# Scores of four key tiles by 512 queries as 26 products instead of two times 14, in 7 of 12 groups

## The chip, the cores and the metric

The kernel runs on one core of one Trainium2 chip, as one program. The metric is the device time of one execution in microseconds (us). A core has a matrix engine (PE) with its weight load (PEld), a vector engine (DVE), a scalar engine (ACT), a general engine (POOL), and SP, which here only issues DMAs. Each engine works through its own queue in the order in which the program wrote it; an instruction that waits holds up everything behind it on that engine. DMAs are issued from the queues of SP and POOL.

## The reference

There are 3327 nodes with 512 features (26 tiles of 128 rows, the last one with 127), and one adjacency matrix. First two rounds of attention over all nodes, then a layer norm, then a binarised layer, then another layer norm:

```python
for l in range(2):
    Wh, Ws = jnp.split(x @ W_stack[l], 2, axis=-1)      # W_stack[l] is 512 by 1024
    a = jax.nn.softmax(Wh @ Ws.T, axis=-1) * adj
    x = leaky_relu(a @ Wh + x, 0.01)
x = layernorm(x0 + x)
x = layernorm(x + relu(adj @ (max(sign(x), 0) @ sign(weight).T)))
```


W_stack is 2 by 512 by 1024. Everything up to the first layer norm is float32. The change concerns the scores `Wh @ Ws.T` of both rounds.

## The kernel before

**The scores as a product of 512 by 512.** With M, the product of the two halves of the weights, a score is a bilinear form of the key's and the query's x. In the stage `project(l)` the kernel makes the query side M x once, in 7 chunks `c` of 512 queries (the last has 256), and in the stage `attention(l)` it multiplies it by the key tiles. For one pair of key tiles `q` (256 keys, 13 pairs) and one chunk, the product is taken as a 2 by 2 block scheme of Strassen's kind: seven block products instead of eight. The left factors ("forms" of the keys) are four raw blocks and four sums (`A11 A12 A21 A22 S1..S4`, of which seven are used), the right ones are `B11 B21 B22 T1..T4`. Each block product has depth 256, that is, two calls of `nc.tensor.matmul` of 128 by 128 by 256. So a pair costs 14 matmul calls, and two pairs (four key tiles) cost 28. Each float32 matmul call stands in the profile as two MATMUL instructions.

**Stage one, `project(l)`.** A chunk `c` is a `weave` of lists: the query side (`queries`, two chains `seven(...)`), the values of two pairs (`project_values`, two chains of `seven`), and `turns`, which are DVE transposes of the next chunk's x (`turn_x`), key sums of the next chunk (`key_sums`), and `prepare` (sums of the next chunk's right factors). `weave` spreads every list evenly over the chunk. Key forms, query forms and value forms are stored to DRAM (`xs_d`, `gs_d`, `ws_d`) by DMAs from the POOL queue: six per pair of key tiles in `keys`, seven per chunk in `queries`.

**Stage two, `attention(l)`.** Two orders run side by side. `steps` is the list of (g, q), 13 groups g of 256 queries by 13 key pairs; step v takes the values: `shift` (subtract the column maximum, DVE), `exponential` (ACT), `running` (sum, DVE), `masked` (times adjacency, DVE), `sums` (four POOL operations of 128x128), then `values`, seven matmul calls into PSUM accumulators. `ahead` is the list of (c, q, s), two half-steps per chunk and key pair; it makes the scores `LOOK` = 30 steps earlier. The loop runs over v, with u = v + LOOK; from v = 0 on, one pass holds seven value matmul calls and eight or six score matmul calls. Within a pass, each operation has a fraction, and `sorted(work, ...)` sets the order in which it is written into every queue: for example `shift` at 0.0, `running` at 0.01, `exponential` at 0.12, `masked` at 0.4, `narrow` (ACT), `degrees` (POOL) and `exact` (DVE) at 0.6 to 0.62 in every second pass, and the scores at

```python
return [(0.06, z1), (0.31, x2), (0.45, add11), (0.56, z6), (0.81, y5)]          # s == 0
return [(0.02, z7), (0.2, add22), (0.35, y3), (0.5, add12), (0.68, z4), ...]    # s == 1
```

The passes with u from 0 to 29 come before v = 0, so they hold scores but no values; they are the scores of chunk 0 and the beginning of chunk 1, in each of the two rounds. The chunk c = 6 has only 256 queries, so its score matmuls are 128 wide.

**How a score leaves PSUM.** The seven products of a pair use three PSUM banks, Z, X and Y (pool `ps_ch`, three buffers). The bank Z is added to by four products in turn; after each, `copied` takes its state out by an ACT copy, and the next product into Z waits for that copy. Per pair there are five ACT copies (three out of Z on the way, one of Y, one as c21) and three DVE adds (`add11`, `add22`, `add12`). Then `maximum` (DVE, 128x512) takes the finished score tile into the column maximum, twice per pair. Score tiles are slots of the ring `s` (`SBUFS` = LOOK + 3).

**Loads.** `load_xs` fetches a pair's key forms two passes ahead (two DMAs, 512 and 384 KB), `load_gs` the next chunk's query forms one by one (double-buffered tile `gs`, 14 KB per partition each), `load_ws` the value forms, `load_adj` the adjacency; all from SP.

## Time and profile before

| | before |
|---|---|
| median of 3 runs | 2530.15 us (2528.65 to 2535.02) |
| the profiled execution | 2530.58 us |
| its span in the profile | 2528.8 us |
| MATMUL instructions | 12237 |

The span is the time from the first to the last instruction on the core; the difference to the execution's time, 1.8 us, lies around it. By position in the span: the first projection ends at 185 us (first score product at 185.1), passes without values run to 277.7, the first round's value steps to about 1228; the second round's first score product is at 1387.5, its first value step at 1480.2, its last near 2423; then comes the binarised layer. In the attention rounds, four passes (two key pairs) take 24.1 to 24.4 us in a chunk of 512 queries, 18.3 to 18.7 us in the chunk of 256, and 12.1 us where there are no values.

A row of the profile's groups reads: line, engine, operation, output <- input, shape, count, busy time in all, mean ns of one, and the idle time of that engine just before it with what ended it. A windows answer gives for each stretch its length, then the busy time of each engine with the number of its instructions in brackets, the granted clock, the share of the DMA engines and GB/s.

### The profile page before, as it was taken

How to read it: one execution, taken by the hardware profiler on the slowest of the kernel's cores; microseconds unless marked ns; L12 is line 12 of the kernel's file. 1: busy time of each engine (PE TensorE's matmuls, PEld its weight loads, DVE VectorE, ACT ScalarE, POOL GpSimd, SP SyncE). 2: the span in 40 equal slices, each digit the busy share in tenths (PEclk: the TensorE clock that was granted, in tenths of full speed). 3: DMA queues.
4: the chain of work that ended last, by engine and by line, in shares of the span. 5: the costliest groups of instructions: out<-in, count | busy, mean ns of one | idle time of the engine just before them, and what ended most of it. 6: DMA issues, size and time to landing. Idle time of an engine off the chain costs nothing.

```text
span 2528.8 us, 39245 instructions
## 1 busy us (share of the span) xinstructions
PE 2505.6 (99%) x12237; PEld 2182.1 (86%) x12237; DVE 2024.0 (80%) x3749; ACT 784.2 (31%) x1822; POOL 1467.6 (58%) x2303
## 2 busy tenths in 40 slices
PE   9999999999999999999999999999999999999998
PEld 7888888888888888998888888888888888899875
DVE  5765778789787897869876587888888888898976
ACT  3323333333333233222232333332323323322234
POOL 3652566766666666556665256666666666655631
PEclk9999999999999999999999999999999999999999
DMA  6857777777767767798885877777777777778984
GB/s 206 298 199 236 229 248 232 247 250 238 248 231 250 246 231 246 249 315 267 256 295 204 254 232 249 244 251 254 239 260 238 255 248 242 248 261 301 316 283 151
DMA packets 311394, 628.83 MB, mean 249 GB/s; under 512 B 35819, under 2 KB 166755, under 8 KB 310924
## 3 DMA queue, kind: packets, MB, share of 16 engines
q1 hardware_dynamic: 278254, 529.13, 64.4%
q0 software_dynamic: 32896, 97.09, 10.4%
q8 instruction: 100, 1.64, 0.3%
q14 instruction: 114, 0.93, 0.1%
q10 hardware_dynamic: 30, 0.03, 0.0%
HBM read 528.54 MB, written 97.58 MB: 248 GB/s over the span
## 4 chain that ended last, share of the span: by engine, by line
PE 93%; DVE 4%; issue 1%; DMA 1%; POOL 1%; ACT 0%; SPq 0%; ACTq 0%; DVEq 0%; POOLq 0%
PE acc L830 37%; PE pZ L596 22%; PE pY L596 11%; PE pX L596 6%; PE pZ_wh L412 4%; PE pZ_g L474 3%; PE agg L1120 3%; PE pY_wh L412 2%; PE pY_g L474 2%; PE pm L316 1%; PE pxw L1212 1%; PE pX_wh L412 1%; PE pX_g L474 1%; DVE s L754 1%; PE pg L449 1%
## 5 line engine op out<-in xcount | busy, mean ns | idle before, releaser
L596 PE MATMUL pZ<-gs,xs 128*128 128x256 f32 (+1 forms) x2912 | 699.4, 364 | 0.6 <-ACT u L614 0.4
L596 PEld LDWEIGHTS pZ<-gs,xs 128*128 128x128 f32 x2912 | 536.2, 190 | 72.6 <-ACT p L614 1.3
L803 POOL TENSOR_TENSOR as<-s 128x128 f32<-128x128 f32 x338 | 169.1, 500 | 592.6 <-DVE s L770 411.5
L830 PE MATMUL acc<-ws,s 128*128 128x256 f32 x1352 | 402.2, 379 | 0.0
L596 PE MATMUL pY<-gs,xs 128*128 128x256 f32 (+1 forms) x1456 | 352.1, 364 | 1.8 <-ACT p L614 1.8
L830 PE MATMUL acc<-ws,as 128*128 128x256 f32 x1352 | 349.5, 380 | 2.0 <-POOL as L805 2.0
L830 PE MATMUL acc<-wh,s 128*128 128x256 f32 x1352 | 349.0, 379 | 0.0
L783 POOL TENSOR_TENSOR deg<-deg,adj 128x256 fp8e4<-128x256 fp8e4 x338 | 280.1, 829 | 52.0 <-DMA adj<-in_adjT_dram 37.6
L662 DVE TENSOR_TENSOR top<-top,s 128x512 f32<-128x512 f32 x286 | 248.1, 873 | 73.1 <-ACT s L649 70.5
L596 PEld LDWEIGHTS pY<-gs,xs 128*128 128x128 f32 x1456 | 268.3, 190 | 37.5 <-ACT p L614 2.6
L754 DVE TENSOR_TENSOR s<-s,off 128x512 f32<-128x512 f32 x338 | 296.0, 876 | 0.6
L830 PEld LDWEIGHTS acc<-ws,as 128*128 128x128 f32 x1352 | 251.2, 190 | 40.4 <-POOL as L805 4.7
L830 PEld LDWEIGHTS acc<-ws,s 128*128 128x128 f32 x1352 | 252.9, 190 | 32.2
L830 PEld LDWEIGHTS acc<-wh,s 128*128 128x128 f32 x1352 | 251.6, 190 | 33.5 <-DVE s L770 0.3
L760 ACT ACTIVATE s<-s 128x512 f32<-128x512 f32 x338 | 213.4, 631 | 194.9 <-DVE s L754 192.5
L765 DVE TENSOR_TENSOR total<-total,s 128x512 f32<-128x512 f32 x312 | 270.0, 865 | 0.0
L614 ACT COPY u<-pZ 128x256 f32<-128x256 f32 (+1 forms) x364 | 129.9, 357 | 422.8 <-PE pZ L596 417.5
L639 DVE TENSOR_TENSOR s<-p,u 128x256 f32<-128x256 f32 (+1 forms) x182 | 86.8, 477 | 215.4 <-ACT u L614 210.2
L770 DVE TENSOR_TENSOR s<-s,adj 128x512 f32<-128x512 f32 x338 | 246.4, 729 | 5.0
L804 POOL TENSOR_TENSOR s<-s 128x128 f32<-128x128 f32 x338 | 233.0, 689 | 26.9
L805 POOL TENSOR_TENSOR as<-s 128x128 f32<-128x128 f32 x338 | 225.4, 667 | 26.5
L806 POOL TENSOR_TENSOR as<-s,as 128x128 f32<-128x128 f32 x338 | 205.6, 608 | 26.5
(195 smaller groups left out, 3454.7 us busy)
## 6 DMA issues: line engine op xcount, KB each, us to landing
ws<-ws_d SPq DMA_DIRECT2D x338, 512.0 KB
xs<-xs_d SPq DMA_DIRECT2D x182, 512.0 KB
adj<-in_adjT_dram SPq DMA_DIRECT2D x351, 256.0 KB
xs<-xs_d SPq DMA_DIRECT2D x182, 384.0 KB
gs_d<-gsp POOLq DMA_DIRECT2D x84, 256.0 KB, 2.9
gs<-gs_d SPq DMA_DIRECT2D x70, 256.0 KB
xs_d<-xT POOLq DMA_DIRECT2D x104, 128.0 KB, 3.3
xs_d<-s POOLq DMA_DIRECT2D x52, 256.0 KB, 3.2
```

The lines of the kernel that those rows point to most:

```text
L412: nc.tensor.matmul(bank, of[LEFT[i]][:, k], wr[RIGHT[i]][:, k], start=(start and k == 0), stop=(k == 1), skip_group_check=True,)
L596: nc.tensor.matmul(ch[bank], xs[c, q, a][:, k], gs[c][:, b, k], start=(start and k == 0), stop=(k == 1), skip_group_check=True,)
L662: nc.vector.tensor_tensor(top[i], top[i], t, ALU.max)
L754: nc.vector.tensor_tensor(s, s, off[g].to_broadcast([P, 2, HW]), ALU.subtract)
L760: nc.scalar.activation(sc[g, q], sc[g, q], AF.Exp)
L765: nc.vector.tensor_tensor(total[g], total[g], sc[g, q], ALU.add)
L770: nc.vector.tensor_tensor(s, s, adj[g, q], ALU.mult)
L783: nc.gpsimd.tensor_tensor(deg[:, g], deg[:, g], adj[g, q][:, a], ALU.add, saturate=False)
L804: nc.gpsimd.tensor_tensor(a21, a21, a22, ALU.add)
L805: nc.gpsimd.tensor_tensor(s2, a21, a11, ALU.subtract)
L806: nc.gpsimd.tensor_tensor(s4, a12, s2, ALU.subtract)
L830: nc.tensor.matmul(acc[g][i // 2][:, i % 2], a[i], b[i], start=(q == 0 and i % 2 == 0), stop=(q == NQ - 1), skip_group_check=True,)
```

## The change

Seven of the 12 groups of four key tiles (`QUADS`: groups 1 to 4 in the first round, 1 to 3 in the second; a group is key pairs 2i and 2i+1) are computed for all seven chunks by another scheme. It has 26 products of depth 128, with left forms `x0` to `x25` and 26 right forms. 16 of the right forms are halves of the seven that exist (`QUERY`), and ten are new (`EXTRA`).

In `project`: the key pairs of such a group no longer store their eight blocks; `quad_sums` makes their forms with 24 POOL operations of 128x128 (`add`, `sub`) and six ACT copies (`one`, `whole`) per group, in the projection's chunk `c` whose key pairs are that group's (c = i), and stores them with two DMAs of 13 forms. `query_sums` makes the ten new right forms with ten DVE operations of 128x256 per chunk (128x128 in the last one) and stores them with five POOL DMAs. The last chunk's store and sums (`done`) and these sums go as `rest` into the next chunk's `turns`. Other pairs store three raw blocks rather than four.

In `attention`: `quad_scores` writes 26 matmul calls at 6.5 per pass over four passes, in the order `ORDER`, into five PSUM tiles P, Q, R, S, T of the same three buffers. Per group there are 17 ACT copies out of PSUM, two ACT copies back into PSUM (`seed`, into Q and P), seven DVE adds with an operand in PSUM (`out`), four DVE adds in SBUF, and four POOL adds of 128x256; the four maxima come at 4.75 to 6.35 passes after the group's start, which is during the next group. Forms are loaded 13 at a time in one DMA (852 KB), from a tile of 14 forms with two buffers. The query forms are in two single tiles `ga` (7) and `gb` (5), which change roles with each chunk: one holds the seven, the other the extras, `load_gs` runs in passes 20 to 24 of the chunk before and in pass 0, `load_ge` in passes 1 to 5. The ring gets two slots more, and the packed bits of the last stage move from a `gs` tile to ring slots.

```diff
+QUADS = ((1, 2, 3, 4), (1, 2, 3))
+ORDER = (11, 8, 3, 23, 14, 16, 12, 22, 9, 1, 25, 20, 4,
+         21, 13, 7, 19, 24, 6, 5, 15, 18, 2, 10, 17, 0)
...
-    SBUFS = LOOK + 3
+    SBUFS = LOOK + 5
...
+    def quad_sums(l, i, pair0, pair1):
...
+        def first():
+            sub(at["x3"], x_(A22, 1, 0), x_(A22, 0, 0))
+            sub(at["x22"], x_(S1, 0, 1), at["x3"])
...
+        def sixth():
+            add(at["x16"], x_(S1, 0, 0), at[4])
+            one(0, 10, x_(S2, 1, 0))
+            whole(0, 11, of[1][S3])
+            nc.gpsimd.dma_start(out=xq_d[l][i, 0], in_=staged[0][:, :13])
...
+    def query_sums(l, c, gs, b12):
...
+        def first():
+            sub(23, gs[B11][:, 0], gs[T3][:, 1])
...
+            store(0, 4)
...
+            if q // 2 in QUADS[l]:
+                return of
             to = xs_d[l][q]
-            for raw in (A11, A12, A21, A22):
+            for raw in (A11, A12, A22):
...
-                weave(one + two, pairs, turns)
+                quad = []
+                if c in QUADS[l]:
+                    quad = quad_sums(l, c, of_pair[2 * c], of_pair[2 * c + 1])
+                weave(one + two, pairs, turns, quad)
...
+        def quad_scores(c, i):
...
+            begins = {11: "P", 8: "Q", 3: "R", 24: "S", 10: "T"}
+            joins = dict(zip(
+                (23, 12, 1, 4, 7, 6, 18, 17, 14, 22, 25, 21, 19, 5, 2, 16, 9, 20, 13, 15, 0),
+                "PPPPPPPPQQQQQQQRRRRST",
+            ))
...
+            place = {r: (n + 0.5) / 6.5 for n, r in enumerate(ORDER)}
+            got = [(at_, lambda r=r: one(r)) for r, at_ in place.items()]
+            for r, b, name in (
+                (11, "P", "c10"), (8, "Q", "c21"), (23, "P", "c11"), (14, "Q", "c01"),
+                (16, "R", 1), (12, "P", "c31"), (22, "Q", 3), (9, "R", 2), (1, "P", "c30"),
+                (25, "Q", 0), (20, "R", 1), (4, "P", "c20"), (7, "P", "c00"), (24, "S", 2),
+                (6, "P", 3), (5, "Q", "c01"), (10, "T", 2),
+            ):
+                got.append((place[r] + 0.03, lambda b=b, name=name: keep_as(b, name)))
+            pool = nc.gpsimd
+            got += [
+                (1.0, lambda: add("c10", "c10", 1, pool)),
+                (1.15, lambda: add("c31", "c31", "c01", pool)),
+                (1.45, lambda: add("c11", "c11", 2, pool)),
+                (2.2, lambda: out("c10", "Q")),
+                (2.4, lambda: seed("Q", 3)),
+                (2.5, lambda: out("c00", "R")),
+                (2.82, lambda: add(0, 0, 2)),
+                (3.05, lambda: add("c00", "c00", 0, pool)),
+                (3.22, lambda: out("c20", "S")),
+                (3.38, lambda: out("c21", "P")),
+                (3.54, lambda: out("c11", "Q")),
+                (3.6, lambda: seed("P", "c30")),
+                (3.85, lambda: out("c30", "P", 0)),
+                (4.005, lambda: out("c31", "T")),
+                (4.1, lambda: add(1, 1, 3)),
+                (4.2, lambda: add("c21", "c21", 2)),
+                (4.3, lambda: add("c01", "c01", 1)),
+            ]
...
-            c, i = divmod(u - 7, 2 * NQ)
-            if 0 <= c < NC - 1 and i % 2 == 0 and i // 2 < 7:
-                load_gs(c + 1, i // 2)
+            c, i = divmod(u, 2 * NQ)
+            if 0 <= c < NC - 1 and 20 <= i < 25:
+                load_gs(c + 1, i - 20)
+            if 0 < c < NC and i == 0:
+                load_gs(c, 5, 2)
+            if 0 <= c < NC and 1 <= i < 6:
+                load_ge(c, i - 1)
```

## The prediction

> **What bounds the kernel now.** I read the engines' busy times and the chain first, then groups by shape, then stretches of the length of four passes, since the change acts on groups of four passes.
>
> ```profile
> PE 2505.6 (99%) x12237; PEld 2182.1 (86%) x12237; DVE 2024.0 (80%) x3749; ACT 784.2 (31%) x1822; POOL 1467.6 (58%) x2303
> PE 93%; DVE 4%; issue 1%; DMA 1%; POOL 1%; ACT 0%; SPq 0%; ACTq 0%; DVEq 0%; POOLq 0%
> ```
>
> PE is the chain. It runs without holes: in the third stretch below it starts 112 MATMULs (4 passes of 14 calls, two MATMULs each) in 24.1 us, 215 ns each, though one "lasts" 379. A call of 256 columns is worth 0.43 us.
>
> ```profile
> L596 PE MATMUL pZ<-gs,xs 128*128 128x256 f32 x2496 | 636.1, 379 | 0.1
> L754 DVE TENSOR_TENSOR s<-s,off 128x512 f32<-128x512 f32 x338 | 296.0, 876 | 0.6
> L639 DVE TENSOR_TENSOR s<-p,u 128x256 f32<-128x256 f32 x156 | 78.5, 503 | 201.8 <-ACT u L614 196.6 <-POOL deg L783 4.5 <-POOL as L806 0.8
> L645 DVE TENSOR_TENSOR s<-pY,u 128x256 f32<-128x256 f32 x156 | 65.4, 419 | 9.3 <-PE pY L596 8.9
> L614 ACT COPY p<-pZ 128x256 f32<-128x256 f32 x156 | 58.2, 373 | 176.8 <-PE pZ L596 176.8
> L803 POOL TENSOR_TENSOR as<-s 128x128 f32<-128x128 f32 x338 | 169.1, 500 | 592.6 <-DVE s L770 411.5 <-PE pY L596 88.3 <-PE acc L830 57.1
> L804 POOL TENSOR_TENSOR s<-s 128x128 f32<-128x128 f32 x338 | 233.0, 689 | 26.9
> L872 POOL TENSOR_TENSOR total<-total 128x256 f32<-128x256 f32 x26 | 24.4, 940 | 0.1
> L218 DVE TENSOR_TENSOR xt<-xT 128x512 f32<-128x512 f32 x12 | 8.2, 684 | 0.0
> ```
>
> Here the prices are to be read, and one more thing: the same DVE shape, 128x512 from two SBUF operands, takes 684 ns in the projection (L218), where POOL runs no tensor operation, and 876 in the attention (L754). POOL's 128x128 sums go from 500 to 689 when they meet DVE. With an operand in PSUM (L645) it stays at 419.
>
> ```profile
> 84.10:108.20 24.10, 24.10 (x113) 21.22 (x112) 19.18 (x41) 7.45 (x20) 13.78 (x23) 1.00 0.87 302
> 595.50:619.90 24.40, 24.40 (x116) 21.45 (x114) 22.60 (x35) 7.59 (x17) 17.30 (x26) 1.00 0.73 246
> 644.10:668.20 24.10, 24.10 (x113) 21.23 (x112) 16.48 (x28) 8.15 (x18) 15.69 (x26) 1.00 0.71 238
> 668.20:692.60 24.40, 24.40 (x115) 21.46 (x115) 21.25 (x38) 7.32 (x17) 15.71 (x25) 1.00 0.79 267
> 1080.50:1098.90 18.40, 18.40 (x115) 16.96 (x114) 12.84 (x23) 4.99 (x14) 9.61 (x17) 1.00 1.07 332
> 1795.60:1820.00 24.40, 24.40 (x116) 21.45 (x115) 22.87 (x41) 7.13 (x16) 16.64 (x26) 1.00 0.78 260
> 1820.00:1844.20 24.20, 24.20 (x114) 21.31 (x113) 22.35 (x36) 7.68 (x17) 16.92 (x27) 1.00 0.80 257
> ```
>
> After the length come PE, PEld, DVE, ACT, POOL. The first row is a projection chunk; then, in the first round's chunk 3, groups i = 1, 3, 4; one group of the narrow chunk; groups 1 and 2 of the second round's chunk 3. What matters is DVE (third pair): 22.6, 16.5, 21.3 and 22.9, 22.4 of 24.2 us. It is second in line, with 1.5 to 3 us to spare in most groups that are changed.
>
> **The change part by part**, against the profiled execution's 2530.6 us (span 2528.8 and 1.8 around it; the runs' median, 2530.15, is 0.4 lower).
>
> *PE work removed.* Two calls per group and chunk, 7 groups x 7 chunks = 98, so MATMULs fall by 196. In six chunks 84 x 0.43 = 36.1 us. In the narrow chunk, 18.4 us less 56 value MATMULs x 0.215 leaves 6.35 us for 56 score MATMULs, 0.227 per call: 14 x 0.227 = 3.2. The sum is 39.3. The narrow 3.2 I leave out: there the DMA share is already 1.07 at 332 GB/s. Bounds 0 to 3.2. So **-36.1**.
>
> *Projection.* Ten DVE sums of 128x256 per chunk, at about 0.42 alone; back to back they overlap a little (a timeline of the projection starts them every 0.34), so I take 0.38: 19.2 + 3.8 = 23.0 of 24.1 us, hidden in chunks without quads. In a chunk with quads POOL loses twelve store DMAs (eight at 0.716, four at 0.556: -7.9), gains seven at 0.55 (+3.9) and 24 sums at 0.50 to 0.69 (12.0 to 16.5): 21.8 to 26.3 of 24.1. For the first time here DVE's sums run beside POOL's. From L218 to L754 a DVE sum slows by 0.19 us with POOL busy for two thirds of the time; about four such sums a pass slow by 0.77 for some 3.9 us of POOL, 0.2 us per us. That is 14 x 0.2 = 2.8 us more for DVE, 25.8 against 24.1. Above: all of POOL's new time that DVE cannot pass, up to 5 us a chunk; below: nothing, since the next chunk's sums are due only at its third product, some 4 us later. I take 2.0 per quad chunk, near the row's 1.7: 7 x 2.0 = **+14** (0 to 35). ACT's six copies lie beside it (7.5 busy of 24.1).
>
> *Passes without values (chunk 0, 7 groups).* Only here does PE follow its own score products at full pace. In the timeline a bank's copy starts 0.47 us after the start of its last MATMUL, lasts 0.37, and the next weight load follows 0.05 later, the matmul 0.20 after that: 1.09, against 5 x 0.215 = 1.07 that two calls in between give. So the copies just fit, as before. Three new loops do not. 21, `out` c10, `seed`, 19: a DVE add starts 0.42 after its last MATMUL, 0.42 + 0.42 + 0.03 + 0.37 + 0.25 = 1.49, 0.42 too late. 18, c21, `seed`, 17: the same, 0.42. 7, copy, c00, then 24 into R's bank: 0.47 + 0.37 + 0.04 + 0.42 + 0.25 = 1.55 against 0.64 and the 0.42 already lost, 0.49. That is 1.33 per group; DVE, some 6 to 9 us busy of 11 here, may have a 0.68 maximum in front, once per group: 1.9. 7 x 1.9 = **+13** (0, if an order in the queues hides it, to 20). In passes with values a call stands between any two score calls, so the same loops have 2.4 to 3.1 us: they cost nothing as long as DVE arrives on time.
>
> *Attention with values, 35 groups of 512 queries.* DVE: out go 2 x (0.503 + 0.419 + 0.418) = 2.7, in come 7 x 0.419 + 4 x 0.503 = 4.9: +2.3. POOL: four adds at 0.94 = +3.8, making 16 to 17 into about 20.5. They slow DVE by 0.2 x 3.8 = 0.8 at least (the row's rate) and by 3.8 at most (every us is added); I take 1.7, nearer to the row, raised because DVE has little idle time left in which POOL could run alone. So +4.0 for DVE per group, against PE's new 24.15 - 0.86 = 23.3. With the rows above, and 18.5 and 15.5 in the two groups of these chunks that are not shown (second of the first round, third of the second):
> first round 26.6, 22.5, 20.5, 25.3: over by 3.3, 0, 0, 2.0; second round 26.9, 26.4, 19.5: over by 3.6, 3.1, 0. Per chunk 5.3 and 6.7, x 5 chunks = 60. DVE may fall behind without PE seeing it only by a little: in pass 2 `shift` and `running` (1.7) stand before `out` c10, and 19 is due 3.1 us into the pass, so a lag above some 0.3 us stalls it; elsewhere it is 1 to 2 us. I let 1.3 us of each of the 20 overruns be caught up in the lighter group behind it (26): **+34** (0, if all is caught up, to 60). ACT, 7.5 + 9 x 0.37 = 10.8 of 23.3, is no bound, but its copies stand behind `exponential`, which waits for `shift`: a late DVE is also a late copy.
>
> On this place the Trainium skill, "SBUF — State Buffer", Who interferes with whom, says that a VectorE instruction with two SBUF inputs and a GpSimd instruction that reads SBUF exclude each other for a whole instruction. The rows agree in kind (684 to 876) but average out at 0.2 us per us. By the rule all 3.8 us would be added, 6.1 per group, and this term would be about 60 + 20 x 2.1 = 102 before anything is caught up.
>
> *The rest.* Narrow chunk: its DVE (12.8 of 18.4) has room: 0. `load_ge` (1.3 MB per chunk of 155 us) beside 250 GB/s: 0; if it arrives late, a few us in chunk 0. Form loads of 852 KB instead of 896 KB, two passes ahead as before: 0. Packed bits in ring slots: 0, hidden behind the values of the last groups.
>
> Sum: 2530.6 - 36.1 + 14 + 13 + 34 = 2555.5. **Forecast 2555 us.**
>
> **Rivals.**
> *Faster: the cover holds.* DVE's overruns are averaged over the chunk (its whole load stays at about 94% of PE's) and the projection hides its sums. Then 2530.6 - 36.1 + 13 = 2508. For it: DVE has 8 us idle in group 3, and the maxima can be late. Against it: 0.3 us of margin in front of `seed`. It decides if the stalls over 49 groups stay under 0.7 us a group.
> *About as before.* Half of the projection's and of the attention's cost: 2530.6 - 36.1 + 7 + 13 + 17 = 2531.5.
> *Much slower: POOL becomes the bound.* Its adds and DVE's exclude each other fully, and lag is never caught up: projection 35, passes without values 20, attention 60: 2530.6 - 36.1 + 115 = 2609. For it: POOL at 20.5 of 23.3 us, with `fresh(1)` waiting for its c10 add. Against it: POOL's sums are due two passes later.
> That PE's work does not shrink is excluded: the list `ORDER` has 26 entries.
>
> **How the numbers follow.** Forecast 0.45 (own range 2538 to 2580), cover holds 0.27, as before 0.10, POOL the bound 0.18. No change is taken as within 0.3%, 2522.5 to 2537.7, about what a measurement here can tell. Faster 0.27, same 0.10, slower 0.45 + 0.18 = 0.63. The range leaves out the lower third of the second case and the upper half of the last: 2505 to 2600.
>
> **What would show it.** MATMULs 12237 - 196 = 12041 whatever the time. PE's hidden waits of now (2 to 4 us in all) become tens of us, released by ACT copies (`seed`) and DVE `out`. Groups 1 of both rounds, 2 of the second and 4 of the first take 24 to 26 us with DVE over 95%, group 3 about 23.3. Chunk 0's groups take 13 us rather than 12.1; quad chunks of the projection 25 to 27 rather than 24.1 with POOL over 90%. The prediction is wrong if DVE's 128x512 operations stay near 876 ns and groups 1 and 4 run in 23.3 us, or if PE waits for DMA of `ge` or the forms.

## The result, and the profile after

The changed kernel takes 2608.47 us (2606.00 to 2610.92) against 2530.14 (2528.65 to 2535.02): a ratio of 1.0306, 95% interval 1.0288 to 1.0324. It is slower, and by more than the forecast of 2555 and than the top of its range, 2600. The profiled execution took 2607.52 us, its span 2605.7.

The page of the changed kernel, first the engines and the chain, then the groups that answer to those shown of before. (L746 is now the Strassen groups' matmul, L786 that of the 26 products, L996 `shift`, L1012 `masked`, L798 the adds in SBUF, on POOL or DVE, L1035 `exact`, L1045 and L1046 `sums`.)

```profile
PE 2503.7 (96%) x12041; PEld 2146.5 (82%) x12041; DVE 2246.8 (86%) x4134; ACT 936.9 (36%) x2305; POOL 1717.6 (66%) x2648
...
PE 66%; DVE 18%; DMA 6%; POOL 4%; issue 3%; ACT 1%; SPq 1%; DVEq 0%; ACTq 0%; POOLq 0%
...
L1045 POOL TENSOR_TENSOR as<-s 128x128 f32<-128x128 f32 x338 | 188.1, 556 | 484.4 <-DVE s L1012 414.8
...
L996 DVE TENSOR_TENSOR s<-s,off 128x512 f32<-128x512 f32 x338 | 298.8, 884 | 0.6
...
L1012 DVE TENSOR_TENSOR s<-s,adj 128x512 f32<-128x512 f32 x338 | 273.1, 808 | 2.6
...
L746 PE MATMUL pZ<-ga,xs 128*128 128x256 f32 (+1 forms) x912 | 212.8, 358 | 0.0
...
L798 POOL TENSOR_TENSOR s<-s,q 128x256 f32<-128x256 f32 (+1 forms) x147 | 132.1, 899 | 51.4 <-ACT q L792 28.9
...
L1035 DVE SCALAR_TENSOR_TENSOR dull<-adj 128x512 fp8e4<-128x512 f32 x169 | 161.7, 957 | 0.1
```

PE's share of the chain falls from 93% to 66%, DVE's rises from 4% to 18%, and 10% is now DMA and POOL. PE issues 12041 MATMULs, 196 fewer, as counted. `masked` goes from 729 to 808 ns and the `exact` test (L1035) from 785 to 957; `shift` stays (876 to 884, its row of before stands in the prediction). The rows of before for the other two:

```profile
L770 DVE TENSOR_TENSOR s<-s,adj 128x512 f32<-128x512 f32 x338 | 246.4, 729 | 5.0
...
L793 DVE SCALAR_TENSOR_TENSOR dull<-adj 128x512 fp8e4<-128x512 f32 x169 | 132.7, 785 | 0.1
```

Stretches of four passes in the changed kernel: in the first round's chunk 3 the groups i = 1, 3, 4, then one group of the narrow chunk, groups 1 and 2 of the second round's chunk 3, and last the projection at the place shown of before (columns as in the table before: length, then PE, PEld, DVE, ACT, POOL, each with its instructions; clock, DMA share, GB/s).

```profile
615.70:642.50 26.80, 24.07 (x111) 20.46 (x110) 20.27 (x36) 10.52 (x26) 21.02 (x31) 1.00 0.69 236
665.80:689.10 23.30, 23.30 (x109) 20.56 (x108) 20.71 (x34) 11.26 (x27) 21.13 (x29) 1.00 0.67 218
689.10:716.60 27.50, 25.13 (x115) 21.18 (x114) 26.81 (x46) 10.28 (x26) 21.39 (x33) 1.00 0.64 215
1114.40:1132.60 18.20, 18.12 (x109) 16.39 (x109) 15.48 (x28) 7.12 (x23) 13.61 (x23) 1.00 1.02 328
1847.50:1872.80 25.30, 24.01 (x111) 20.53 (x110) 23.94 (x41) 10.07 (x25) 19.94 (x30) 1.00 0.77 268
1872.80:1898.70 25.90, 24.09 (x109) 20.31 (x108) 25.33 (x41) 10.57 (x26) 22.52 (x32) 1.00 0.62 209
84.10:108.20 24.10, 23.18 (x108) 20.05 (x107) 23.86 (x45) 8.36 (x25) 19.50 (x38) 1.00 0.68 249
```

Group 3 runs in 23.3 us, the saving in full. Group 4 is what the prediction described: DVE busy 26.8 of 27.5 us. But group 1 of the first round takes 26.8 us with DVE busy for only 20.3 and POOL for 21.0. No engine is full there. What holds it is in the list of waits of the changed kernel (engine, what it was to write, line, what released it; total us, times, longest). The first row has one of its longest waits in this stretch: ACT stands for 5.1 us until 635.9.

```profile
ACT ab L1020 <- DMA adj_d<-ab: 54.7, 26, 6.0
...
PEld pQ L786 <- ACT pQ L795: 21.1, 20, 3.4
...
PE pY L746 <- DMA ga<-gs_d: 13.3, 10, 3.0
PE pQ L786 <- ACT pQ L795: 13.1, 16, 3.0
...
PEld pS L786 <- DVE s L801: 12.4, 23, 1.1
PEld pS L786 <- ACT q L792: 12.3, 4, 3.9
...
PE pS L786 <- ACT q L792: 10.7, 4, 3.5
```

PE waits for ACT's copies (`seed`, into PSUM, is L795, `keep_as`, out of it, L792), and ACT waits, in `narrow` (L1020, which turns a block of the adjacency into 8-bit numbers), for a transfer: the store (`keep_blocks`, L1028) of the block before the last, which holds one of `narrow`'s two buffers until it is out. The list of before had the same wait, small:

```profile
ACT ab L778 <- DMA adj_d<-ab: 14.6, 4, 4.6
```

One such place in the timeline of the changed kernel (start, duration, engine, line, operation; in brackets the idle time before it and what ended it):

```profile
1029.63 0.55 POOL L1028 DMA_DIRECT2D adj_d<-ab  x1
...
1033.64 0.41 DVE L801 TENSOR_TENSOR s<-pQ,s 128x256 f32<-128x256 f32 x1
...
1035.18 0.62 ACT L1020 CAST ab<-adj 128x512 fp8e4<-128x512 f32 x1 [4.28 <-DMA adj_d<-ab]
...
1035.70 0.37 ACT L795 COPY pP<-s 128x256 f32<-128x256 f32 x1
1036.01 0.36 ACT L792 COPY q<-pT 128x256 f32<-128x256 f32 x1
1036.12 0.30 PEld L786 LDWEIGHTS pP<-gb,xs 128*128 128x128 f32 x2 [3.59 <-ACT pP L795]
```

POOL issues the store at 1029.63. ACT stands in `narrow` for 4.28 us until that store has left the buffer. The seed of bank P is queued behind it on ACT, and PE's product into P stands still for 3.59 us. Matching each `narrow` with its store through the trace, POOL issued the store 7.40 us after the end of `narrow` before the change, 8.89 after it, and 8.08 without POOL's four adds (experiment 1; medians of 169). The transfer takes another 3.9 to 4.0 us. So a buffer is free again 11.4 us after `narrow` filled it before the change and 13.3 us after it (medians). In all 26 places ACT wants the buffer again after 9.1 to 14.5 us, since blocks stand there in neighbouring passes; where it wants it later (the median over all blocks is 19 us) nothing waits. The 4 waits of before (10.5 to 13.0 us) have become 26: at the crowded places the margin was nearly used up already.

**Where the 76.9 us of span went.** From the starts of the value matmuls, pass by pass, against those of before: projections +7.1 and +6.7; passes without values +5.2 and +4.3; attention with values +22.0 in the first round and +31.4 in the second; end +0.4 (sum 77.1, rounded terms). Of the attention, +13.8 is the narrow chunk and +39.6 the five chunks of 512 queries. These should have gained 35 x 0.86 = 30.1, so what they lost to stalls is about 70 us.

The mean length of a stretch of four passes over chunks 2 to 5, us. The first line is what PE's MATMULs would need without a stall. (A Strassen group spreads its score MATMULs 16, 12, 16, 12 over four passes and a group of 26 products 14, 12, 14, 12; where one kind follows the other a pass holds 8 or 16. So stretch 0 is shorter as well, and the last stretch of a row of changed groups is as long as before.) The lines below that of the changed kernel are experiments 3, 9 and 6.

| | round 1: 0 | 1 | 2 | 3 | 4 | round 2: 0 | 1 | 2 | 3 |
|---|---|---|---|---|---|---|---|---|---|
| without a stall | 23.3 | 23.5 | 23.3 | 23.3 | 24.4 | 23.3 | 23.5 | 23.3 | 24.2 |
| before | 24.2 | 24.4 | 24.2 | 24.2 | 24.4 | 24.2 | 24.4 | 24.2 | 24.2 |
| changed | 24.2 | 25.5 | 23.8 | 23.3 | 28.2 | 24.5 | 25.7 | 26.9 | 24.4 |
| store issued by SP | 24.0 | 23.5 | 23.9 | 23.3 | 25.8 | 24.2 | 24.8 | 26.1 | 24.2 |
| and `exact` left out | 24.1 | 23.5 | 23.6 | 23.3 | 25.1 | 24.2 | 24.3 | 23.9 | 24.3 |
| forms in rotating places | 23.3 | 26.6 | 23.9 | 23.3 | 29.3 | 23.3 | 25.7 | 27.0 | 24.4 |

### The profile page after: what moved, and what is told of

Read it like the earlier page. It is cut to its first block, busy times and chain, and to the rows that moved or that the text cites. A ratio compares the mean times of both kernels' runs of the same rounds, so it can differ in the third digit from the quotient of the medians.

```text
span 2605.7 us, 39761 instructions
## 1 busy us (share of the span) xinstructions
PE 2503.7 (96%) x12041; PEld 2146.5 (82%) x12041; DVE 2246.8 (86%) x4134; ACT 936.9 (36%) x2305; POOL 1717.6 (66%) x2648
## 4 chain that ended last, share of the span: by engine, by line
PE 66%; DVE 18%; DMA 6%; POOL 4%; issue 3%; ACT 1%; SPq 1%; DVEq 0%; ACTq 0%; POOLq 0%
PE acc L1072 27%; PE pZ L746 9%; PE pY L746 4%; PE pP L786 4%; PE pQ L786 3%; DMA ga<-gs_d 3%; PE agg L1375 3%; PE pX L746 2%; PE pZ_wh L535 2%; DVE s L996 2%; DVE s L1012 2%; PE pR L786 2%; DMA adj_d<-ab 2%; DVE total L1007 2%; PE pZ_g L599 2%
## 5 line engine op out<-in xcount | busy, mean ns | idle before, releaser
L1045 POOL TENSOR_TENSOR as<-s 128x128 f32<-128x128 f32 x338 | 188.1, 556 | 484.4 <-DVE s L1012 414.8
L1072 PE MATMUL acc<-ws,as 128*128 128x256 f32 x1352 | 378.0, 381 | 2.0 <-POOL as L1047 2.0
L1072 PE MATMUL acc<-wh,s 128*128 128x256 f32 x1352 | 377.2, 380 | 0.0
L996 DVE TENSOR_TENSOR s<-s,off 128x512 f32<-128x512 f32 x338 | 298.8, 884 | 0.6
L1012 DVE TENSOR_TENSOR s<-s,adj 128x512 f32<-128x512 f32 x338 | 273.1, 808 | 2.6
L1048 POOL TENSOR_TENSOR as<-s,as 128x128 f32<-128x128 f32 x338 | 225.3, 667 | 26.5
L1046 POOL TENSOR_TENSOR s<-s 128x128 f32<-128x128 f32 x338 | 215.9, 639 | 26.8
L746 PE MATMUL pZ<-ga,xs 128*128 128x256 f32 (+1 forms) x912 | 212.8, 358 | 0.0
L1072 PE MATMUL acc<-wh,as 128*128 128x256 f32 x676 | 203.2, 383 | 0.0
L746 PEld LDWEIGHTS pZ<-ga,xs 128*128 128x128 f32 x912 | 165.9, 191 | 21.4 <-issue 0.7
L792 ACT COPY s<-pP 128x256 f32<-128x256 f32 (+1 forms) x294 | 105.1, 357 | 213.4 <-PE pP L786 210.2
L798 POOL TENSOR_TENSOR s<-s,q 128x256 f32<-128x256 f32 (+1 forms) x147 | 132.1, 899 | 51.4 <-ACT q L792 28.9
L1035 DVE SCALAR_TENSOR_TENSOR dull<-adj 128x512 fp8e4<-128x512 f32 x169 | 161.7, 957 | 0.1
```

The costliest lines, as they stand in the source:

```text
L746: nc.tensor.matmul(ch[bank], xs[c, q, a][:, k], query(c, b)[:, k], start=(start and k == 0), stop=(k == 1), skip_group_check=True,)
L996: nc.vector.tensor_tensor(s, s, off[g].to_broadcast([P, 2, HW]), ALU.subtract)
L1012: nc.vector.tensor_tensor(s, s, adj[g, q], ALU.mult)
L1046: nc.gpsimd.tensor_tensor(a21, a21, a22, ALU.add)
L1048: nc.gpsimd.tensor_tensor(s4, a12, s2, ALU.subtract)
L1072: nc.tensor.matmul(acc[g][i // 2][:, i % 2], a[i], b[i], start=(q == 0 and i % 2 == 0), stop=(q == NQ - 1), skip_group_check=True,)
```

## The experiments

**1. Without POOL's four adds.**

```diff
-                (1.0, lambda: add("c10", "c10", 1, pool)),
-                (1.15, lambda: add("c31", "c31", "c01", pool)),
-                (1.45, lambda: add("c11", "c11", 2, pool)),
...
-                (3.05, lambda: add("c00", "c00", 0, pool)),
```

> The four POOL adds of each group (into c10, c31, c11, c00) are left out, nothing else; these scores lack one term. PE's holes in the passes with values are about 95 us in the changed kernel (2608). Theory A (POOL: its adds hold up DVE's operations on SBUF operands, and fill POOL so that what stands behind them on it is late): at least half of the holes go, time 2550 to 2565, the mean of DVE's L1012 falls back from 808 toward 729 ns, and ACT's waits for the store adj_d (54.7 us) fall to about 15. Theory B (DVE's own five more adds per group and the new loops through DVE and ACT are enough to stall PE): less than 20 us is gained, time above 2588, with the same waits of PE for the copies into Q and P.

2562.89 us (2557.62 to 2567.72), ratio 1.0124 (1.0102 to 1.0146): 45.6 less than the changed kernel. POOL's busy time falls to 1551.4 us, ACT's wait for the store from 54.7 to 21.9, and the mean of `masked` to 763 ns. So more than half of the loss hangs on POOL's four adds; whether by its time, by DVE that it slows, or by what it issues late is open at this point.

**2. The same four adds on DVE.**

```diff
-            pool = nc.gpsimd
+            pool = nc.vector
```

> The same four adds per group run on DVE instead of POOL, at the same places in the order; the result is the same. DVE gets 196 more adds of 128x256, about 0.4 to 0.5 us each, some 1.8 us per group of 23 us; POOL loses 0.9 each. Theory A (an add on POOL costs DVE its whole time, about 0.9 us, while DVE needs half of that itself): 2570 to 2590, faster than 2608. Theory B (DVE's load is what counts): DVE is over 100% in the loaded groups, 2620 to 2650.

2579.08 us (2578.48 to 2585.90), ratio 1.0197 (1.0178 to 1.0217): 29 less, although DVE, the engine that the prediction called full, gets 196 operations more. Its busy time hardly moves (2249.7 against 2246.8 us), since `masked` falls from 808 to 745 ns. ACT's wait for the store is 25.9.

**3. The store of the packed block from SP's queue instead of POOL's.**

```diff
-            nc.gpsimd.dma_start(out=adj_d[g][:, q], in_=adj.pop((g, q, "b")))
+            nc.sync.dma_start(out=adj_d[g][:, q], in_=adj.pop((g, q, "b")))
```

> The store of the narrowed adjacency block (adj_d) is issued from SP's queue instead of POOL's; all else as changed. Theory C (POOL is behind, so it issues this store late; the next narrowing on ACT waits for its buffer, and the copies into P and Q stand behind it): the 54.7 us that ACT waits for the store fall below 15, and 20 to 35 us of PE's holes go: 2573 to 2588. Rival (ACT's wait is beside the point, since DVE is late at the same places): within 8 us of 2608.

2568.38 us (2567.90 to 2569.76), ratio 1.0148 (1.0131 to 1.0165): 40 less, somewhat more than was expected of the late store. All arithmetic is on the engine where it was, and `masked` still takes 807 ns. But DVE is busy for 30 us less (2216.8 against 2246.8): `exact` falls from 957 to 856 ns and `shift` from 884 to 851. The list of waits of this kernel has

```profile
ACT ab L1020 <- DMA adj_d<-ab: 10.6, 8, 2.0
```

and its stretches for group 1 and 4 of the first round and 2 of the second, chunk 3, are

```profile
604.20:627.70 23.50, 23.50 (x111) 20.68 (x110) 20.10 (x36) 10.65 (x26) 19.74 (x26) 1.00 0.81 274
...
674.80:700.40 25.60, 24.91 (x115) 21.27 (x114) 25.09 (x46) 10.41 (x26) 20.71 (x28) 1.00 0.69 228
...
1843.10:1870.70 27.60, 25.34 (x110) 21.41 (x109) 26.38 (x42) 10.67 (x26) 22.49 (x30) 0.94 0.63 211
```

Group 1 loses its stall altogether (26.8 to 23.5, with DVE at the same 20 us). The groups with a full DVE, 25.1 of 25.6 and 26.4 of 27.6 us, keep theirs. (In the last stretch the granted clock was 0.94, so a part of its length is the clock's; its mean over four chunks is 26.1.) Here is what is left, in the timeline of this kernel:

```profile
1856.92 0.94 DVE L996 TENSOR_TENSOR s<-s,off 128x512 f32<-128x512 f32 x1
1857.78 0.94 DVE L1007 TENSOR_TENSOR total<-total,s 128x512 f32<-128x512 f32 x1
...
1858.64 0.41 DVE L801 TENSOR_TENSOR s<-pQ,s 128x256 f32<-128x256 f32 x1
...
1859.14 0.38 ACT L795 COPY pQ<-q 128x256 f32<-128x256 f32 x1 [0.62 <-DVE s L801]
...
1859.57 0.30 PEld L786 LDWEIGHTS pQ<-gb,xs 128*128 128x128 f32 x2 [2.08 <-ACT pQ L795]
```

DVE, without a gap before, does `shift`, `running`, then `out` c10; the seed of Q follows, and PE has waited 2.08 us. This is the loop that the prediction named for pass 2.

**4. No group by the 26 products, all else of the change kept.**

```diff
-QUADS = ((1, 2, 3, 4), (1, 2, 3))
+QUADS = ((), ())
```

> No group uses the 26 products (QUADS empty), but the ten extra query sums per chunk, their stores and loads, and the new tiles ga and gb with their later loads stay. PE has its 12237 MATMULs again. If the extra sums alone fit beside PE in the projection, and the loss there comes from the key sums on POOL and DVE's slowing by them, the projections take what they took before (185 us to the first score product) and only the late loads of two query forms at the start of each chunk cost, about 1.2 us per wide chunk and 3 to 4 for the narrow one: 2545 to 2550. If the extra sums alone are the projection's loss (14 us in both rounds): 2555 to 2565.

2548.47 us (2541.67 to 2550.76), ratio 1.0060 (1.0039 to 1.0081): the surroundings of the change cost 18 us by themselves, as the first expectation had it. By stage, against before: 2.6 in the passes without values, 4.4 in the wide chunks and 7.7 in the narrow one; nothing in the projections. The first score product comes 3.0 us later, but so does the first projection chunk (at 42.2 instead of 39.2 us), and from there to the first score product it is 145.9 us in both rounds, as before the change: the ten DVE sums and their stores fit. The start before that chunk lies between 38.7 and 42.2 us in the traces of all fourteen kernels, and it moves with unchanged code as well (39.2 in the kernel before, 41.0 in experiment 12), so these 3.0 us, and 1.2 at the end, are hardly the change's. The wide and the narrow chunks' losses are mostly PE waiting for the forms 5 and 6 of the next queries (`load_gs`, 9.6 us in the list of waits), which are now loaded at a chunk's first pass. One such place in the changed kernel's timeline, at the start of the narrow chunk:

```profile
2311.24 0.96 SPq L723 DMA_DIRECT2D ga<-gs_d  x2
...
2318.40 1.19 PE L746 MATMUL pY<-ga,xs 128*128 128x128 f32 x4 [2.93 <-DMA ga<-gs_d]
```

Seven microseconds after the issue PE still waits. In this kernel the new `ge` sums on DVE take 419 ns; beside POOL's key sums, in the changed kernel, the same form takes 523.

**5. Four buffers for the packed block instead of two**, paid for with one slot of the ring; the store stays on POOL.

```diff
-    SBUFS = LOOK + 5
+    SBUFS = LOOK + 4
...
-                [P, 2, HW], F8, tag="adj_b", bufs=2, name=f"ab_{l}_{g}_{q}"
+                [P, 2, HW], F8, tag="adj_b", bufs=4, name=f"ab_{l}_{g}_{q}"
```

> Four buffers instead of two for the narrowed adjacency block, the store stays on POOL's queue with all its work there; the ring has one slot less, which makes the room and can only cost. It tells apart why the store from SP's queue gave 40 us. Theory C1 (the late store holds the narrowing on ACT, and the copies behind it): the same gain comes with POOL's work unchanged, 2565 to 2580. Theory C2 (POOL was relieved of 169 issues of 0.55 us): little is gained, 2595 to 2610.

2589.94 us (2588.14 to 2591.85), ratio 1.0236 (1.0219 to 1.0253): 18.5 less, between the two expectations. ACT's wait for the store is gone from the list, and the attention gains 24 us; 2.9 are lost again in the two projections, perhaps by the ring's missing slot, and 2.2 in the start before them. So the buffer explains 24 of the 37 us by which the attention gains when SP issues the store. The other 13 are not from the wait for the buffer. One thing that SP's issue changes and the buffers do not is DVE's time: 2250.0 us here, 2216.8 there. The kernel before has it too, 2024.0 us and 1997.0 with the store on SP (experiment 12). That these 30 us are the 13 is likely, since experiment 9 shows DVE's time to count in the full groups, but it was not tried alone.

**6. The query forms in places that rotate**, so that forms 5 and 6 of the next chunk go where two forms of this one are done with, and are loaded at pass 25 of this chunk instead of pass 0 of the next.

```diff
+        seven_at, five_at = [list(range(7))], [list(range(7, 12))]
+        for _ in range(1, NC):
+            old7, old5 = seven_at[-1], five_at[-1]
+            seven_at.append(old5 + old7[:2])
+            five_at.append(old7[2:])
...
-            if 0 < c < NC and i == 0:
-                load_gs(c, 5, 2)
+            if 0 <= c < NC - 1 and i == 25:
+                load_gs(c + 1, 5, 2)
```

> The places of the query forms rotate from chunk to chunk, so that the two forms that are loaded last go where the old B11 and B21 were, which are free one pass earlier; their loads are issued one pass earlier. The same result. PE waits 18 us for these loads in the changed kernel. Theory D (they are late only because their places come free late): most of it goes, 2592 to 2600. Rival (the DMA engines are full at that point, above all in the narrow chunk): the wait moves to other loads, 2603 to 2610.

2599.96 us (2595.28 to 2604.52), ratio 1.0275 (1.0257 to 1.0293): 8.5 less, just inside the first expectation. PE's wait for `ga<-gs_d`, 13.3 us in the list and some 15 from one MATMUL's start to the next over its ten places (the expectation's 18 was too much), is gone, and stretch 0 of both rounds is at its 23.3 us. But stretches 1 and 4 of the first round grew by 1.1 each. That is mostly the clock (last section): its record has ten spells of half clock in this execution, nine of 3.41 us and one of 6.83, 37.6 us together, where that of the changed kernel has five, 20.5 us. Half of the difference, 8.5 us, is what they can cost; with the 8.5 gained it makes 17, near the 15 of the waits. In chunks 2 to 5 of the first round the changed kernel has one such spell, this one five, all in stretches 1 and 4.

**7. Store on SP and adds on DVE together.**

```diff
-            pool = nc.gpsimd
+            pool = nc.vector
...
-            nc.gpsimd.dma_start(out=adj_d[g][:, q], in_=adj.pop((g, q, "b")))
+            nc.sync.dma_start(out=adj_d[g][:, q], in_=adj.pop((g, q, "b")))
```

> The store on SP's queue and the four adds on DVE together. Alone they gave 40 and 29 us. If both act by keeping POOL's store in time, they are one effect: 2560 to 2572. If the store is one cause and the shared time of POOL's and DVE's operations on SBUF another, they add up: 2540 to 2552.

2569.40 us (2565.55 to 2572.67), ratio 1.0149 (1.0132 to 1.0166), the same as the store alone. `masked` is down to 732 ns, as before the change, and it gives nothing: DVE does the four adds in the time that it no longer loses beside POOL's. So 40 and 29 us were largely two ways to the same thing, a POOL that does not issue the store late.

**8. POOL loaded again, with the store on SP**: two POOL memsets per block, which no one waits for.

```diff
+            scr = att.tile([P, HW], F8, tag="scr", bufs=1, name=f"scr_{l}_{g}_{q}")
+            for _ in range(2):
+                nc.gpsimd.memset(scr, 0.0)
+            nc.sync.dma_start(out=adj_d[g][:, q], in_=adj.pop((g, q, "b")))
```

> The store on SP's queue as in the run that gave 40 us (2568), and in its place on POOL two memsets of 128x256 bytes that nobody waits for, to give POOL back about the time of the 169 issues (0.55 us each). If relieving POOL was part of the 40 us (four buffers for the block, with the store left on POOL, gave 18), the time rises to 2578 to 2590. If only the late store mattered, it stays within 6 of 2568.

2574.01 us (2570.20 to 2581.23), ratio 1.0176 (1.0159 to 1.0194): 5.6 more than with the store on SP alone. The page of this kernel shows what went in, 0.62 us a block for the 0.55 of issuing that left POOL:

```profile
L1030 POOL MEMSET scr<- 128x256 fp8e4 x338 | 105.2, 311 | 9.7
```

Of the 6.0 us between the two profiled executions, 4.0 lie in the start and the end of the kernel, where there are no memsets. So nearly all of the 40 us, 34 at least, are from where and when the store is issued, and POOL's relief is 2 us or nothing (the two intervals overlap). The memsets take POOL's time, but they do not slow DVE as the issues do (2224.2 us busy, against 2216.8 without them and 2246.8 with the issues), so this run does not speak against DVE's part in the 40 us.

**9. DVE relieved, with the store on SP**: the `exact` test, one DVE operation of 128x512 every two passes, left out.

```diff
-            nc.gpsimd.dma_start(out=adj_d[g][:, q], in_=adj.pop((g, q, "b")))
+            nc.sync.dma_start(out=adj_d[g][:, q], in_=adj.pop((g, q, "b")))
...
-            nc.vector.scalar_tensor_tensor(
-                dull, at, 0.0, at, ALU.is_gt, ALU.not_equal, accum_out=cnt[:, i : i + 1],
-                saturate=False,
-            )
```

> The store on SP's queue, and the DVE operation that tests the adjacency entries (exact, 0.8 to 0.96 us in every second pass) left out; the test for other values than 0 and 1 is then missing. With the store on SP, 40 us of PE's holes in the passes with values remain, most in groups 1 and 2 of the second round and 4 of the first. Theory E (DVE's sum of work in the loaded groups is the bound): 1.8 us of DVE less per group takes most of it, 2536 to 2548. Rival F (the loops out, seed, next product are too tight whatever DVE's load): 2558 to 2568.

2549.62 us (2547.21 to 2552.47), ratio 1.0073 (1.0058 to 1.0089): 18.8 less than with the store alone, a little short of what was expected for DVE's load as the cause. It comes from the stretches with a full DVE: in the table, group 2 of the second round goes from 26.1 to 23.9, group 1 from 24.8 to 24.3, group 4 of the first from 25.8 to 25.1; group 3, with room, stays at 23.3. DVE's load is the second cause. (POOL is busy for 62 us less as well, 1612.1 against 1674.2, with the same instructions; what `exact` costs by its own time and what by slowing POOL is not told apart.)

**10. The 26 products only in four groups with room**, together with the diffs of experiments 6 and 7.

```diff
-QUADS = ((1, 2, 3, 4), (1, 2, 3))
+QUADS = ((1, 2, 3), (3,))
```

> Store on SP, adds on DVE, rotating places, and the 26 products only in the groups where DVE had room before: 1, 2, 3 of the first round and 3 of the second. Four groups, each with 5 x 0.86 in the wide chunks that have values, 0.4 in the narrow one, less 0.5 in chunk 0: about -17 us. Against it the projection (3 for the extra sums, 1 to 2 for each group's sums, 8 in all), late loads that remain (3) and the first loads of chunk 0 (6). So 2526 to 2538: as before or a little faster.

2523.65 us (2521.20 to 2524.86, ten runs) against 2529.98: ratio 0.9974 (0.9964 to 0.9983). That is below the 2526 to 2538 that were expected. It beats both kernels, the one before by 0.26%, which is just inside what the prediction called no change, with an interval that leaves 1 out. The page has PE back where it was:

```profile
PE 2488.4 (99%) x12125; PEld 2158.7 (86%) x12125; DVE 2159.4 (86%) x4141; ACT 875.2 (35%) x2098; POOL 1449.9 (58%) x2238
...
PE 93%; DVE 4%; issue 1%; DMA 1%; ACT 1%; POOL 0%; DVEq 0%; ACTq 0%; SPq 0%; POOLq 0%
```

A wide chunk of the first round with three such groups is 2.4 us shorter than before, one of the second with one group 0.9: 0.8 to 0.9 a group, the two calls that PE saves. The first projection takes back 5.6 of it, counted from its first chunk, the second nothing, and the passes without values 3.8.

**11. The same with POOL's key sums (`quad_sums`) on DVE.**

```diff
-            nc.gpsimd.tensor_tensor(to, a, b, ALU.subtract)
+            nc.vector.tensor_tensor(to, a, b, ALU.subtract)
...
-            nc.gpsimd.tensor_tensor(to, a, b, ALU.add)
+            nc.vector.tensor_tensor(to, a, b, ALU.add)
```

> The version with few groups (2523.7), with the 24 key sums per group in the projection on DVE instead of POOL. If POOL's sums cost DVE their own time where they meet (about 0.45 us each against 0.2 on DVE), the projections lose less than the 5 us that they lose now: 2519 to 2523. If DVE's own time is what counts (24 more operations in a chunk where it is 99% busy): 2526 to 2535.

2527.09 us (2524.06 to 2529.79), ratio 0.9985 (0.9976 to 0.9994): 3.4 more than experiment 10. Counted from their first chunk, the two projections cost 8.6 and 1.0 us instead of 5.6 and nothing. There the sums are better on POOL, though they slow DVE's.

**12. The kernel before with only its store moved to SP**, the line of experiment 3 in the kernel before.

```diff
-            nc.gpsimd.dma_start(out=adj_d[g][:, q], in_=adj.pop((g, q, "b")))
+            nc.sync.dma_start(out=adj_d[g][:, q], in_=adj.pop((g, q, "b")))
```

> The kernel before, with only the store of the narrowed block on SP's queue. PE has no holes there, so nothing is gained: 2528 to 2532. If it is faster by more than 4 us, the gain of the version with few groups comes from this store and not from the 26 products.

2530.41 us (2528.55 to 2531.44), ratio 0.9995 (0.9986 to 1.0004). Before the change the store's place costs nothing, so the gain of experiment 10 is the products', and the 40 us of experiment 3 are a cost that the change switched on.

## Why the prediction was wrong, point by point

- *PE work removed, 36.1 us*: right. 12041 MATMULs, and where nothing stands in the way a stretch shrinks by 0.86 to 0.9 us (group 3; experiment 10).
- *Projection, +14*: right, +13.8; counted from their first chunk the two take 7.4 and 6.7 us longer, for four and three groups, so 2.0 a group, as was forecast. The way was right too: the ten sums alone are hidden (experiment 4), and with POOL's key sums beside them DVE is full (23.9 of 24.1 us in the row above). POOL stood at 19.5 to 21.9, below the 90% that was to show it.
- *Passes without values, +13*: 15.5 (9.5 net and 6.0 saved), and made otherwise. Groups 2 to 4 take 12.6 us; without a stall 12.09 - 0.86 = 11.23, so the three loops cost 1.37, near the 1.33 that was worked out; the extra 0.57 for DVE's queue did not come. Groups 0 and 1 take 14.4 and 13.7, since PE waits for its first staged keys (`xs<-xq_d`, 2.2 and 0.7 us in the first round), for which the prediction had no term; that the loads of the query forms beside them make them late is likely: experiment 4, which has these loads and no group of 26 products, waits 0.98 us for keys at the same place in the first round, and the kernel before does not wait there. The prediction said of `load_ge` "if it arrives late, a few us in chunk 0", and took 0.
- *Attention with values, +34 (0 to 60)*: this is the step that failed: about 70. The part that it was made of, DVE over its time, came out about right in sum. With the store on SP, groups 1 and 4, and 1 and 2 of the second round, stall for 0, 1.4, 1.3 and 2.8 us, 5.5 per pair of chunks and 27 over five pairs, where 34 was forecast, and the timeline shows the named loop. Group by group the sum was wrong, and that its total came near is partly luck: a group's four maxima (3.5 us of DVE) now run during the next group, as the description of the change says, so the first changed group of a row is relieved and not loaded. Group 1 was to have 26.6 us of DVE and has 20.1 with the store on SP. The sentence that was wrong is "ACT … is no bound, but its copies stand behind `exponential`". They stand behind `narrow` as well, which has two buffers, and whose store is issued by POOL; with POOL's new work that store was issued 1.5 us later, and the margin was used up. The price of the store's place is about 37 us in the attention (53.4 net with the store on POOL, 16.6 with it on SP), of which the wait for the buffer is 24 (experiment 5). The prediction asked who waits for POOL's results and answered that "POOL's sums are due two passes later"; it did not ask who waits for what POOL issues.
- Group 1 of the first round was forecast as 23.3 + 3.3 = 26.6 by an overloaded DVE, and one such group took 26.8, for the other reason: DVE was busy for 20.3 us, and with the store on SP the group takes 23.5. The length alone would have confirmed a wrong cause. Group 4's overrun was taken against 23.3, where PE itself has 24.4 (115 MATMULs, as before).
- *Narrow chunk 0, form loads 0*: wrong, +13.8 in the narrow chunk, 7.7 of it there without any of the 26 products (experiment 4), and up to 5.1 by two spells of half clock in the second round's. The prediction saw the DMA share of 1.07 in this chunk but let `load_gs` for forms 5 and 6 move from the chunk before into the first pass without asking when they are due. PE waiting for the forms was among its own signs of being wrong, and that sign came: 13.3 us for these and 5.8 for the staged keys.
- *The clock*: no term of the prediction. At most half of 20.5 us, 10, went to it (last section); it is part of the 70 and the 13.8.
- *The rivals*: 2608 is the time of "POOL becomes the bound" (2609), but not its mechanism. That gave 35 to the projection and 60 to DVE and POOL excluding each other. Experiment 7 removes that exclusion for the four adds and gains nothing beyond the store; experiment 8 loads POOL again and loses 6 at most.

What stays open: where the 13 us come from that SP's issue gains over two more buffers (experiment 5); DVE's 30 us are the likely place.

## What to carry to other kernels

Before an engine is given more work, list what its queue issues as well as what it computes: a store that sits behind the new work holds its buffer longer, and the next engine that needs the buffer stands still with all that is queued behind. A small wait with few counts in the list of before (here 4 waits, 14.6 us, on an engine that is 31% busy) is the sign that this margin is nearly used up. And a change that gains in stretches with room and loses in those without is worth splitting: four of the seven groups, with store, adds and form loads mended, gained 0.26%, where all seven cost 3% and, with store and adds mended, still 1.5% (all seven with all three were not run).

## What was not expected of the hardware

**A stall of PE can cost as much again in clock.** Stretches of the changed kernel before, in, at once after and later after a stall, columns as above (PEclk is third from the end):

```profile
2045.00:2049.00 4.00, 3.69 (x18) 2.91 (x16) 3.97 (x5) 1.28 (x4) 3.77 (x6) 1.00 0.58 197
2049.00:2051.50 2.50, 1.13 (x4) 0.68 (x4) 2.50 (x5) 0.68 (x2) 2.40 (x4) 1.00 0.79 251
2051.90:2055.30 3.40, 3.40 (x8) 2.78 (x9) 3.29 (x7) 0.74 (x2) 3.15 (x8) 0.51 0.34 136
2055.30:2058.00 2.70, 2.70 (x14) 2.37 (x14) 1.28 (x3) 1.41 (x3) 1.16 (x2) 1.00 0.69 197
```

After two weight loads that stand 1.95 us apart, PE starts 8 MATMULs in 3.4 us at a granted clock of 0.51, then 14 in 2.7. It counts as busy there, so no list of waits shows this loss. From 100 us on, 21 pairs of weight loads of the changed kernel stand over 1.9 us apart; five such stalls, of 2.0 to 3.6 us, were followed by half clock, four times for 3.41 us and once for 6.83 by the trace's clock record, and others up to 4.1 us were not. The kernel before has two such pairs and that of experiment 10 four, and neither has such a spell before its last 12 us. The Trainium skill, "TensorE: Matmul & The Clock Gate", Part 1, tells of a gate that halves the clock after an idle window of about 3.4 us and watches in windows that run freely, whatever the kernel does. The length agrees, and so do the free windows: in every trace of this case that has more than one spell, they begin whole multiples of 3.413 us apart. That the window must be idle differs from the rows, and they decide. Windows cut by these starts, the first followed by half clock, the other two not:

```profile
2048.38:2051.79 3.41, 1.44 (x6) 0.68 (x4) 3.41 (x6) 1.30 (x3) 3.31 (x5) 1.00 0.85 271
...
1031.18:1034.59 3.41, 1.75 (x8) 0.91 (x6) 3.41 (x6) 0.00 (x0) 2.60 (x5) 1.00 0.99 365
1034.59:1038.00 3.41, 1.88 (x9) 1.68 (x10) 1.42 (x5) 1.20 (x3) 3.15 (x6) 1.00 0.20 76
```

The stall of 1.95 us lies in one window and leaves PE 1.44 us of work in it; one of 3.78 us at 1032 is split over two and leaves 1.75 and 1.88. In all fourteen traces (both kernels and the twelve experiments), from 100 us to the last matmul, 49 windows at full clock are followed by half clock, and in each of them PE or its weight load was busy for 1.66 us or less of the 3.41; in none of the 9952 others was it less than 1.43. So what counts is how much of one such window a stall empties, and by where the windows fall, a stall of 2 us may cost clock and one of 4 us may not.

**A two-input operation of DVE can stand still through several operations of POOL.** In the changed kernel's timeline, `exact` on DVE, 785 ns on average before the change, and POOL beside it:

```profile
698.81 3.21 DVE L1035 SCALAR_TENSOR_TENSOR dull<-adj 128x512 fp8e4<-128x512 f32 x1
698.96 0.73 POOL L1114 TENSOR_TENSOR total<-total 128x256 f32<-128x256 f32 x1
699.64 0.73 POOL L798 TENSOR_TENSOR s<-s,q 128x256 f32<-128x256 f32 x1
...
700.33 0.72 POOL L798 TENSOR_TENSOR s<-s,s 128x256 f32<-128x256 f32 x1
701.01 0.45 POOL L1045 TENSOR_TENSOR as<-s 128x128 f32<-128x128 f32 x1
```

It lasts 3.21 us, where the shortest of its kind take 0.68, and ends 0.56 after the last of four operations of POOL that run back to back. The Trainium skill states in "SBUF — State Buffer", Who interferes with whom, that a DVE instruction with two SBUF inputs contends with a GpSimd instruction that reads SBUF, and that the port pair they share is an exclusive lock. The row agrees for this instance; as a rate, every microsecond of POOL added to DVE, it does not hold, since the mean of the 169 went only from 785 to 957 ns, that of `masked` from 729 to 808, and that of `shift` from 876 to 884, with 250 us more of POOL's busy time. So four adds of 0.9 us on POOL cost about the same on DVE (experiment 7 against 3: 2569.4 and 2568.4 us, DVE busy for 2228.3 and 2216.8): what DVE spends in running them itself it had mostly been losing beside them.
